# Attention scores from one product of 308 columns and two of 154, and a re-ordered slot, fill and end

## The chip, the cores and the metric

The kernel runs on one core of a Trainium2 chip. The metric is the device time of one launch in microseconds (us), lower is better; several executions of each kernel are timed and their median is compared. Besides, one execution was taken with the hardware profiler; the profile's numbers are of that execution.

## The reference, cut to what matters

Cross attention of `x` (32 batches, 512 queries, 640 channels) with a context of 77 rows of 1024 channels per batch, in 20 heads of 32 channels, float32 throughout. The text has 77 rows, so the object, other and image slices of the context are empty and only the text attention counts.

```python
q = heads(x @ to_q_w)                       # 32 x 20 x 512 x 32
k, v = heads(ctx @ to_k_w), heads(ctx @ to_v_w)   # 32 x 20 x 77 x 32
p = softmax(einsum('bhqd,bhkd->bhqk', q, k) / sqrt(32))
out = merge(einsum('bhqk,bhkd->bhqd', p, v)) @ to_out_w + to_out_b + x
```

## The kernel before

**Number format.** Every matrix product is done in the type fp32r. A float32 operand is first split into a high part (a cast to fp32r, ScalarE, `nc.scalar.copy`) and a low part (the rest, a subtraction, VectorE or GpSimd), and a product of two operands is the sum of three products, `PAIRS` (L127): high by high, high by low, low by high. A low by low product is left out. A product on TensorE (PE) is a weight load of a 128x128 tile (PEld) and a matmul that streams up to 512 columns through it into a PSUM bank.

**First stage** (to about 270 us): the keys and values of all batches are made from the context in column groups of 512, split, and written to DRAM: `k_dram` [128 channels, 5 chunks, 2 parts, 2464 keys] by `split_keys` (L207) and `v_dram`. The high part stands first. Two tiles `ks` take turns, and one DMA writes both parts of one chunk and group; it is issued by GpSimd, for the last group by SyncE (SP).

**Main stage**: 160 slots, `slot(n)` (L661). Slot n works for batch b = n // 5 and chunk j = n % 5; a chunk is 128 channels, that is 4 heads. A batch is thus 5 slots, j = 0 to 4. The order of all instructions on each engine is the order in which the program writes them (`manual_schedule`, L267); no scheduler moves them, and each engine takes its instructions in that order. In one slot there are, with the lines of the profile:

- scores for four blocks t of 128 queries, `scores(n, t)` (L448): three products of 308 columns (4 heads x 77 keys). The stationary operand is a block of the queries `qt` (parts high and low), the moving one is `kb`, which has the keys of head i in rows 32i to 32i+31 and columns 77i to 77i+76 and zeros elsewhere, in a high and a low copy. VectorE (DVE) takes the maximum of each head (L462).
- `exps(n, t)` (L467): four exponentials with their sums on ScalarE (ACT, L472).
- `queries(n + 1)` (L429): 15 products of 512 columns into the one bank `pq`; `split_q(n + 1)` (L443) casts it to `qt` on ACT (L103) and subtracts on DVE (L104). Two tiles `qt` take turns.
- `normalize(n - 1)` on GpSimd (POOL, L487), `transpose_p(n - 1)` on DVE (L494) and four DMAs from its output `z` to a scratch `pd` in DRAM; `load_p(n - 2)` loads it back in another layout as `raw` (L510, L511).
- for the slot that lies `LAG` = 3 back: `cast_p` (ACT, L518), `rest_p` (ACT L524 and DVE L525), `last_p` (POOL, L532), then `values` (six products of 512 columns into `pa`, L546), `sum_a` (ACT L557, DVE L559), and in the next slot `high_a` (ACT L566) and `low_a` (DVE L571).
- 24 products of 320 columns of the output projection of an earlier batch in two pieces, `piece` (L604, L589), into two banks `po` that take turns; `finish` (L612) adds each closed bank to the residual `xr` on DVE (L618), which frees the bank, and issues the DMA of a complete row block.
- `add_bias` (POOL, L582) on a loaded residual, at the places that `BIAS` (L635) names: j = 2, 3, 4 and 0.
- `refill` (L648): the keys or values of the next part, from SP's queue. `load_keys` (L411) issues one DMA for each head.
- the next batch's `x`: loads from SP, transposes on DVE (L256), and in j = 2 and 3 five splits (`split_x`, L258: ACT cast L263, POOL subtraction L264).

On ACT, DVE and POOL the order of a slot is, cut to what the prediction follows:

```
ACT : cast_p, high_a, rest_p, exps 0, exps 1, cast of qt, exps 2, [x casts], sum_a, [x casts], exps 3
POOL: last_p (waits for rest_p's cast), normalize(n - 1), [add_bias], [x subtractions]
DVE : rest_p, low_a, maxima 1 and 2, transpose_p(n - 1), low part of qt, maximum 3, finish, sum_a
PE  : scores 0, queries, scores 1, queries, scores 2, piece, values, scores 3, piece
```

In j = 3 the first piece and its `finish` stand ahead of `transpose_p`. Slots 3 to 6 are "filling": there is an older slot to take, but no projection yet; in these `cast_p`, `rest_p` and `last_p` follow `exps(n, 1)` and the first half of `refill` follows `load_p`.

**End**: `end()` (L771) takes the last three slots' values and projects what is left.

## Time and profile before

| | |
|---|---|
| median of 3 runs | 1954.53 us (1954.48 to 1955.75) |
| the profiled execution | 1951.98 us, span 1949.9 us, granted TensorE clock 0.994 |
| PE busy | 1905.3 us (98%), 10332 products |
| ACT, DVE, POOL busy | 1533.9, 1437.6, 1015.2 us (79, 74, 52%) |
| score products (L454) | 1920 of 128x308, mean 305 ns from start to modelled end |
| low part of `qt` (L104) | 160 of 128x512, mean 654 ns |
| cast of `qt` (L103) | 160 of 128x512, mean 598 ns |
| DMA | 431.28 MB, 560919 packets, 187024 of them under 512 B |

The profile has 40 slices of the span, groups of instructions by line, the waits of each engine with what ended them, and the instructions in order of time. A product's duration overlaps those of its neighbours, so the price of a product is read from one start to the next. SPq is SyncE's queue, which issues the DMAs; an issue there also takes time.

### The profile page before, as it was taken

What the parts mean: (1) busy time and instruction counts of PE and PEld (TensorE: products, weight loads), DVE (VectorE), ACT (ScalarE), POOL (GpSimd) and SP (SyncE); (2) the same over time, 40 slices, a digit from 0 to 9 for tenths busy, and PEclk for the clock granted to TensorE, in tenths of its full rate; (3) what the DMA queues carried; (4) which work ended last, traced back from release to release, by engine and by line L of the source; (5) the groups of instructions that cost most, each with busy time, mean ns of one, the idle gap of its engine ahead of it and who ended that gap; (6) DMA issues with size and microseconds to landing.
All of it is one profiled execution on the core that took longest, in us unless ns stands there. A gap on an engine that the chain in (4) does not pass through costs nothing.

```text
span 1949.9 us, 36251 instructions
## 1 busy us (share of the span) xinstructions
PE 1905.3 (98%) x10332; PEld 1701.3 (87%) x10332; DVE 1437.6 (74%) x2334; ACT 1533.9 (79%) x6210; POOL 1015.2 (52%) x668
## 2 busy tenths in 40 slices
PE   9999998999999999999999999999999999999997
PEld 7787896889889989988889989988989999888896
DVE  4444345887888788787888878788888888877874
ACT  3232237898988898888888888898989989888982
POOL 1100055566556655555556555566655665556543
PEclk9999999999999999999999999999999999999999
DMA  9878878888888888988888888888889888888874
GB/s 185 190 188 232 201 198 215 222 226 230 228 225 230 227 229 228 239 232 218 227 238 233 229 225 228 236 232 224 228 232 237 227 229 225 225 224 232 230 201 144
DMA packets 560919, 431.28 MB, mean 221 GB/s; under 512 B 187024, under 2 KB 469072, under 8 KB 560720
## 3 DMA queue, kind: packets, MB, share of 16 engines
q1 hardware_dynamic: 556208, 414.46, 82.3%
q0 software_dynamic: 4416, 14.34, 2.2%
q8 instruction: 84, 1.38, 0.3%
q14 instruction: 115, 0.94, 0.2%
q10 hardware_dynamic: 96, 0.16, 0.0%
HBM read 247.17 MB, written 181.64 MB: 220 GB/s over the span
## 4 chain that ended last, share of the span: by engine, by line
PE 20%; ACT 19%; issue 17%; DMA 15%; DVE 13%; POOL 12%; SPq 2%; DVEq 0%; POOLq 0%; ACTq 0%
ACT pn L472 10%; POOL pn L487 8%; DMA raw<-pd 7%; DMA pd<-z 6%; PE pq L435 5%; PE po L589 5%; POOL pp L532 4%; DVE pp L525 3%; ACT xt L263 3%; ACT aw L557 3%; PE pk L191 2%; PE pv L191 2%; PE sc L454 2%; DVE nm L462 2%; DVE z L494 2%
## 5 line engine op out<-in xcount | busy, mean ns | idle before, releaser
L472 ACT ACTIVATE pn<-sc,nm 128x77 f32<-128x77 f32 x2560 | 802.5, 335 | 70.9 <-DVE nm L462 68.0
L589 PE MATMUL po<-wo_s,at 128*128 128x320 f32 x3840 | 624.3, 310 | 17.7 <-DVE xr L618 14.4
L435 PE MATMUL pq<-xt,wq_s 128*128 128x512 f32 x2400 | 605.4, 393 | 0.0
L589 PEld LDWEIGHTS po<-wo_s,at 128*128 128x128 f32 x3840 | 575.4, 188 | 27.8 <-DVE xr L618 24.6
L532 POOL TENSOR_TENSOR pp<-raw,pp 64x512 fp32r<-64x512 f32 x160 | 211.8, 1324 | 643.6 <-ACT pp L524 413.4
L472 ACT ACTIVATION_READ_ACCUMULATOR pn<-sc,nm 128x1 f32 x2560 | 545.1, 213 | 0.0
L435 PEld LDWEIGHTS pq<-xt,wq_s 128*128 128x128 f32 x2400 | 436.8, 188 | 75.1
L454 PE MATMUL sc<-kb,qt 128*128 128x308 f32 x1920 | 377.5, 305 | 1.3 <-ACT pn L472 0.5
L487 POOL TENSOR_TENSOR pn<-pn,rs 128x1232 f32<-128x1232 f32 x160 | 364.4, 2277 | 24.7 <-DVE rs L482 12.6
L494 DVE STREAM_TRANSPOSE z<-pn 128x1280 f32<-128x1280 f32 x160 | 241.8, 1511 | 168.8 <-POOL pn L487 158.4
L454 PEld LDWEIGHTS sc<-kb,qt 128*128 128x128 f32 x1920 | 325.7, 189 | 45.0 <-ACT pn L472 1.6
L462 DVE TENSOR_REDUCE nm<-sc 128x4 f32<-128x308 f32 x640 | 295.1, 462 | 46.4 <-PE sc L454 44.1
L546 PE MATMUL pa<-pp,vb 128*128 128x512 f32 x960 | 256.0, 401 | 10.5 <-ACT pp L518 4.8
L525 DVE TENSOR_TENSOR pp<-raw,pp 128x1024 fp32r<-128x1024 f32 x160 | 195.6, 1222 | 88.2 <-ACT pp L518 78.9
L559 DVE TENSOR_TENSOR pa<-pa,aw 64x512 f32<-64x512 f32 x320 | 222.6, 696 | 34.7 <-ACT aw L557 25.2
L557 ACT COPY aw<-pa 64x1024 f32<-64x1024 f32 x160 | 162.0, 1012 | 79.6 <-PE pa L546 77.4
L264 POOL TENSOR_TENSOR xt<-xs,xt 128x512 fp32r<-128x512 f32 x160 | 204.3, 1296 | 37.1 <-ACT xt L263 35.3
L546 PEld LDWEIGHTS pa<-pp,vb 128*128 128x128 f32 x960 | 175.3, 190 | 43.8 <-ACT pp L518 5.8
L582 POOL TENSOR_TENSOR xr<-xr,bias 128x640 f32<-128x640 f32 x128 | 201.5, 1575 | 0.2
L518 ACT CAST pp<-raw 128x1024 fp32r<-128x1024 f32 x160 | 168.9, 1055 | 33.0 <-DMA raw<-pd 33.0
L191 PE MATMUL pk<-ct,wk_s 128*128 128x512 f32 (+1 forms) x600 | 137.9, 388 | 9.1 <-ACT ct L103 6.4
L191 PEld LDWEIGHTS pk<-ct,wk_s 128*128 128x128 f32 x600 | 114.2, 191 | 31.1 <-ACT ct L103 7.3
(43 smaller groups left out, 1358.0 us busy)
## 6 DMA issues: line engine op xcount, KB each, us to landing
pd<-z SPq DMA_DIRECT2D x640, 160.0 KB, 3.8
raw<-pd SPq DMA_DIRECT2D x160, 512.0 KB, 4.0
xs<-in_x_dram SPq DMA_DIRECT2D x128, 320.0 KB, 6.2
xr<-in_x_dram SPq DMA_DIRECT2D x128, 320.0 KB, 4.1
out_dram<-xr SPq DMA_DIRECT2D x127, 320.0 KB, 4.1
raw<-pd SPq DMA_DIRECT2D x160, 128.0 KB, 4.2
v_dram<-vs SPq DMA_DIRECT2D x80, 192.0 KB, 3.9
k_dram<-ks POOLq DMA_DIRECT2D x20, 512.0 KB, 3.7
```

The source lines that it names most:

```text
L191: nc.tensor.matmul(held[j][:, :gn], w[:, k, a, :], cts[g, k][:, c, :gn], start=(k == 0 and n == 0), stop=(k == NK - 1 and n == 2),)
L435: nc.tensor.matmul(pqs[n], wq_s[:, k, a, j * P : (j + 1) * P], xts[b, k][:, c, :], start=(k == 0 and m == 0), stop=(k == NC_ - 1 and m == 2),)
L454: nc.tensor.matmul(sc[:, :KCOLS], qt[:, a, t * P : (t + 1) * P], kb[:, j - GROUPS[g][0], c], start=(m == 0), stop=(m == 2),)
L462: nc.vector.tensor_reduce(nm, sc[:, :KCOLS].rearrange("p (h k) -> p h k", k=NKEY), AX.X, ALU.max, negate=True)
L472: nc.scalar.activation(pnb[n % 2][:, at, :NKEY], sc[:, i * NKEY : (i + 1) * NKEY], AF.Exp, bias=nm[:, i : i + 1], accum_out=sms[n][:, at : ...
L487: nc.gpsimd.tensor_tensor(pf, pf, rs.unsqueeze(2).to_broadcast([P, NQ * HPC, NKEY]), ALU.mult)
L494: nc.vector.transpose(z.rearrange("p b t j -> p t b j"), pn.rearrange("p (t h) k -> p t (h k)", t=NQ).rearrange("p t (b i) -> p t b i", i=Q),)
L525: nc.vector.tensor_tensor(pp[:, 2:4, :], raw[:, 0:2, :], pp[:, 0:2, :].bitcast(F32), ALU.subtract)
L532: nc.gpsimd.tensor_tensor(pp[64:, 4, :], raw[:64, 2, :], pp[:64, 4, :].bitcast(F32), ALU.subtract)
L546: nc.tensor.matmul(pas[n][:, p, :], vb[:, p, t, :], pp[:, c, :], start=(c == p), stop=(t == 1),)
L559: nc.vector.tensor_tensor(pa[64 * p : 64 * p + 64, 0], pa[:64, p], aw[:, p], ALU.add)
L589: nc.tensor.matmul(pos[b, t, h][:, :HALF], ats[b * NC_ + j][:, a, t * P : (t + 1) * P], wos[0][:, j, c, h * HALF : (h + 1) * HALF], start= ...
```

## The change

The high by low and the low by high product have the same rows half empty: rows of heads 0 and 1 meet only columns 0 to 153, rows of heads 2 and 3 only columns 154 to 307. The new score tile is one product of 308 columns (high by high, as before) and two of 154 columns: the first holds, for heads 0 and 1, the low queries in rows 0 to 63 and the high queries, copied, in rows 64 to 127, against a key tile `kc` with their high keys in rows 0 to 63 and their low keys in rows 64 to 127; the second does the same for heads 2 and 3 with the two halves of the rows exchanged. `qt` has three parts instead of two: the high queries and two mixed ones. GpSimd makes the two copies (64 rows by 512 columns each, to the other half of the partitions), and the subtraction on DVE becomes two of 64 rows.

`kb` keeps the high keys alone, `kc` holds both parts at half width: the bytes in SBUF are the same. `load_keys` issues two DMAs for each head. The two parts of `k_dram` now are the two pairs of heads, each with its high keys in one half of the rows and its low keys in the other, so `split_keys` issues three DMAs instead of one.

In a slot, `add_bias` is moved: for j = 2 and 3 (and in the last slot) ahead of `scores(n, 0)`, for j = 4 and 0 behind `split_q`. In j = 0, too, the first piece and its `finish` now come ahead of `transpose_p`. In the filling slots `cast_p`, `rest_p` and `last_p` stand where the other slots have them. In `end()`, `piece(last - 1, 6)` with its `finish` is moved to the start and `transpose_p(N - 1)` behind the second `finish`.

```diff
@@ -209,9 +209,10 @@
         ks = kvt.tile([P, 2, G], FPR, tag="ks", name="ks")
         split(ks[:, 0, :gn], ks[:, 1, :gn], pks.pop(j)[:, :gn])
         engine = nc.gpsimd if g + 1 < len(GROUPS_KV) else nc.sync
-        engine.dma_start(
-            k_dram[:, j, :, g0 : g0 + gn].bitcast(F32), ks[:, :, :gn].bitcast(F32)
-        )
+        dst = k_dram.rearrange("(h r) c w n -> r c w h n", h=2)[:, j, :, :, g0 : g0 + gn]
+        engine.dma_start(dst[:, 0].bitcast(F32), ks[:64, :, :gn].bitcast(F32))
+        for half in range(2):
+            engine.dma_start(dst[:, 1, half].bitcast(F32), ks[64:, 1 - half, :gn].bitcast(F32))
 
     def values_of(g, j, pool):
 
@@ -394,14 +395,16 @@
     nc.sync.dma_start(bias, bo.unsqueeze(0).to_broadcast([P, C]))
     kbs, vbs, pnb = [], [], []
     for g, (j0, nj) in enumerate(GROUPS):
-        kb = main.tile([P, nj, 2, KCOLS], FPR, name=f"kb{g}")
-        nc.gpsimd.memset(kb.bitcast(F32), 0.0)
-        kbs.append(kb)
+        kb = main.tile([P, nj, KCOLS], FPR, name=f"kb{g}")
+        kc = main.tile([P, nj, 2, KCOLS // 2], FPR, name=f"kc{g}")
+        for tile_ in (kb, kc):
+            nc.gpsimd.memset(tile_.bitcast(F32), 0.0)
+        kbs.append((kb, kc))
     for n in range(2):
         pn = main.tile([P, NQ * HPC, KPAD], F32, name=f"pn{n}")
         nc.gpsimd.memset(pn, 0.0)
         pnb.append(pn)
-    qts = [main.tile([P, 2, S], FPR, name=f"qt{n}") for n in range(2)]
+    qts = [main.tile([P, 3, S], FPR, name=f"qt{n}") for n in range(2)]
     z = main.tile([P, NBLK, NQ, Q], F32, name="z")
     for g, (j0, nj) in enumerate(GROUPS):
         vb = main.tile([P, nj, 2, 2, P], FPR, name=f"vb{g}")
@@ -410,10 +413,14 @@
 
     def load_keys(b, g, heads=range(HPC)):
         j0, nj = GROUPS[g]
+        kb, kc = kbs[g]
         src = k_dram[:, j0 : j0 + nj, :, b * NKEY : (b + 1) * NKEY].bitcast(F32)
         for i in heads:
-            r = slice(i * HD, (i + 1) * HD)
-            nc.sync.dma_start(kbs[g][r, :, :, i * NKEY : (i + 1) * NKEY].bitcast(F32), src[r])
+            r, half = slice(i * HD, (i + 1) * HD), i % 2 * NKEY
+            nc.sync.dma_start(
+                kb[r, :, i * NKEY : (i + 1) * NKEY].bitcast(F32), src[r, :, i // 2, :]
+            )
+            nc.sync.dma_start(kc[r, :, :, half : half + NKEY].bitcast(F32), src[r])
 
     def load_values(b, g, segments=SEGMENTS):
         j0, nj = GROUPS[g]
@@ -443,18 +450,34 @@
     def split_q(n):
 
         qt, pq = qts[n % 2], pqs.pop(n)
-        split(qt[:, 0, :], qt[:, 1, :], pq)
+        nc.scalar.copy(qt[:, 0, :], pq)
+        lower, upper = slice(0, 64), slice(64, P)
+        halves = ((lower, upper), (upper, lower))
+        for w, (r, other) in enumerate(halves):
+            nc.gpsimd.tensor_copy(qt[other, 1 + w, :], qt[r, 0, :].bitcast(F32))
+        for w, (r, other) in enumerate(halves):
+            nc.vector.tensor_tensor(
+                qt[r, 1 + w, :], pq[r], qt[r, 0, :].bitcast(F32), ALU.subtract
+            )
 
     def scores(n, t):
         b, j = divmod(n, NC_)
         g = GROUP_OF[j]
-        qt, kb = qts[n % 2], kbs[g]
+        qt, (kb, kc) = qts[n % 2], kbs[g]
+        jg = j - GROUPS[g][0]
         sc = ps.tile([P, S], F32, tag="sc", name="sc", bufs=3)
-        for m, (a, c) in enumerate(PAIRS):
+        half = KCOLS // 2
+        for m, (cols, keys_) in enumerate(
+            (
+                (slice(0, KCOLS), kb[:, jg]),
+                (slice(0, half), kc[:, jg, 0]),
+                (slice(half, KCOLS), kc[:, jg, 1]),
+            )
+        ):
             nc.tensor.matmul(
-                sc[:, :KCOLS],
-                qt[:, a, t * P : (t + 1) * P],
-                kb[:, j - GROUPS[g][0], c],
+                sc[:, cols],
+                qt[:, m, t * P : (t + 1) * P],
+                keys_,
                 start=(m == 0),
                 stop=(m == 2),
             )
@@ -672,15 +695,18 @@
         filling = taken is not None and not has_out
         if not filling:
             refill(b, j, 0)
-        if taken is not None and not filling:
+        if taken is not None:
             cast_p(taken)
         if n - 1 in takes:
             high_a(takes[n - 1])
+        bias_now = j in BIAS and b >= BIAS[j][0]
+        if bias_now and (j in (2, 3) or not ahead):
+            add_bias(b - BIAS[j][0], BIAS[j][1])
         s = scores(n, 0)
-        if taken is not None and not filling:
+        if taken is not None:
             rest_p(taken)
         rs = sums(n - 1) if n else None
-        if taken is not None and not filling:
+        if taken is not None:
             last_p(taken)
         if n:
             normalize(n - 1, rs)
@@ -704,13 +730,7 @@
             load_x(b + 2, (0, 1))
         if j in RESIDUAL and b >= RESIDUAL[j][0]:
             load_residual(b - RESIDUAL[j][0], RESIDUAL[j][1])
-        if j in BIAS and b >= BIAS[j][0]:
-            add_bias(b - BIAS[j][0], BIAS[j][1])
         exps(n, 1, *s)
-        if filling:
-            cast_p(taken)
-            rest_p(taken)
-            last_p(taken)
         for i in turns[0]:
             transpose_x(b + 1, i)
         if ahead:
@@ -720,13 +740,16 @@
             exps(n, 2, *s)
             piece(bo_, first)
             s = scores(n, 3)
-        if j == 3 and has_out:
+        early = ahead and has_out and j in (0, 3)
+        if early:
             piece(bo_, first)
             finish()
         if n and has_out:
             transpose_p(n - 1)
         if ahead:
             split_q(n + 1)
+            if bias_now and j not in (2, 3):
+                add_bias(b - BIAS[j][0], BIAS[j][1])
             exps(n, 2, *s)
         if n and not has_out:
             transpose_p(n - 1)
@@ -743,7 +766,7 @@
             sum_a(taken)
             return
         if has_out:
-            if j != 3:
+            if not early:
                 piece(bo_, first)
         else:
             s = scores(n, 3)
@@ -773,17 +796,17 @@
 
         last = B - 1
         load_p(N - 2)
-        transpose_p(N - 1)
+        piece(last - 1, 6)
+        finish()
         high_a(N - 4)
+        cast_p(N - 3)
         low_a(N - 4)
-        cast_p(N - 3)
         rest_p(N - 3)
         last_p(N - 3)
         add_bias(last - 1, 3)
-        piece(last - 1, 6)
-        finish()
         piece(last - 1, 7)
         finish()
+        transpose_p(N - 1)
         load_p(N - 1)
         load_residual(last, 0)
         load_residual(last, 1)
```

## The prediction

> **What bounds the kernel now.** I read the page first, then the stretches of the span, the waits in the steady part (420 to 1850 us), and the instructions of single slots in order of time.
>
> ```profile
> PE 1905.3 (98%) x10332; PEld 1701.3 (87%) x10332; DVE 1437.6 (74%) x2334; ACT 1533.9 (79%) x6210; POOL 1015.2 (52%) x668
> ```
>
> ```profile
> 420.00:1850.00 1430.00, 1421.48 (x7993) 1285.25 (x7993) 1153.84 (x1881) 1279.23 (x5332) 851.07 (x535) 1.00 0.87 229
> ```
>
> ```profile
> DVE z L494 <- POOL pn L487: 142.3, 129, 2.0
> ...
> ACT pp L518 <- DMA raw<-pd: 31.1, 28, 2.3
> PEld po L589 <- DVE xr L618: 16.1, 29, 1.2
> ```
>
> The second line has the busy us of PE, PEld, DVE, ACT and POOL in the steady part: PE 1421 of 1430. A batch has 285 products (75 + 60 + 120 + 30), so 7993 of them are 28.05 batches of 50.98 us. The last three lines (waits: us, times, longest) say that PE is not alone: once a batch it waits for a bank (0.57 us; without it PE would need 50.4), and once a batch the first cast of a slot waits 1.1 us for `raw`. So a second thing runs at nearly PE's pace. It is seen in one slot with j = 1: ACT and POOL, then DVE, then PE.
>
> ```profile
> 899.28 1.05 ACT L518 CAST pp<-raw 128x1024 fp32r<-128x1024 f32 x1 [1.81 <-DMA raw<-pd]
> ...
> 901.46 1.29 POOL L532 TENSOR_TENSOR pp<-raw,pp 64x512 fp32r<-64x512 f32 x1 [6.60 <-ACT pp L524]
> ...
> 902.83 2.27 POOL L487 TENSOR_TENSOR pn<-pn,rs 128x1232 f32<-128x1232 f32 x1
> ...
> 907.64 0.33 ACT L472 ACTIVATE pn<-sc,nm 128x77 f32<-128x77 f32 x1 [0.84 <-DVE nm L462]
> ...
> 908.86 1.06 ACT L518 CAST pp<-raw 128x1024 fp32r<-128x1024 f32 x1
> ```
>
> ```profile
> 905.14 1.51 DVE L494 STREAM_TRANSPOSE z<-pn 128x1280 f32<-128x1280 f32 x1 [0.95 <-POOL pn L487]
> 906.57 0.65 DVE L104 TENSOR_TENSOR qt<-pq,qt 128x512 fp32r<-128x512 f32 x1
> 907.15 0.46 DVE L462 TENSOR_REDUCE nm<-sc 128x4 f32<-128x308 f32 x1
> ```
>
> ```profile
> 905.27 0.59 PE L454 MATMUL sc<-kb,qt 128*128 128x308 f32 x3
> 905.71 1.93 PE L589 MATMUL po<-wo_s,at 128*128 128x320 f32 x12
> 907.47 0.59 PE L454 MATMUL sc<-kb,qt 128*128 128x308 f32 x3
> 907.90 1.55 PE L435 MATMUL pq<-xt,wq_s 128*128 128x512 f32 x6
> ```
>
> This is a ring: casts of `raw` on ACT (899.28 to 901.46: 2.18), `last_p` (1.37), normalise (2.31), transpose (1.43), low part of `qt` (0.58), maximum 3 (0.49), exponentials 3 (1.22), and the next slot's cast at 908.86. Each step starts as the one before ends; the sum is 9.58. The maximum had its scores at about 905.9 and still waited for the subtraction ahead of it on DVE. The next casts start at 919.20, 929.52, 939.11 and 950.42 (the last after 1.62 of waiting for `raw`): steps of 10.34, 10.32, 9.59 and 9.69. In j = 3 ACT's casts of x come last, with 0.8 to spare for the maximum; in j = 2 up to 0.3. The ring without its `raw` wait is 49.5 us a batch against PE's 50.4, and with it 51.1.
>
> **Part by part.**
>
> *Score products.* From start to start in the rows above: 308 columns (907.90 - 907.47)/3 = 0.143, 320 columns 1.76/12 = 0.147. With 0.231 for 512 columns (15 in a slot), a column costs 0.44 ns, and 154 columns would cost 75 ns. But each has its own weight load, and where PE restarts after a wait, loads follow one another faster than products:
>
> ```profile
> 307.99 0.19 PEld L454 LDWEIGHTS sc<-kb,qt 128*128 128x128 f32 x1 [0.79 <-ACT pn L472]
> 308.10 0.19 PEld L454 LDWEIGHTS sc<-kb,qt 128*128 128x128 f32 x1
> 308.24 0.19 PEld L454 LDWEIGHTS sc<-kb,qt 128*128 128x128 f32 x1
> ```
>
> The second load starts 0.11 after the first though PE was idle: no row shows loads closer than this. I take 0.115 for a product of 154 columns, with ends 0.075 and 0.231 (the widest row; nothing under 308 columns is in the trace, so dearer than 308 is not excluded). A score tile goes from 0.429 to 0.143 + 2 x 0.115 = 0.373, and 640 tiles take 36 us off PE (87 at 0.075, 45 at 0.108; 111 us more at 0.231); PE would need 50.4 - 20 x 0.056 = 49.3 a batch. The Trainium skill, "TensorE: Matmul & The Clock Gate", section "Back-to-back issue gap", gives columns/2.4 + 2.5 ns for the isolated gap, 67 ns for 154 columns, which would make it 82 us; the row for 308 columns (143 where the rule has 131) and the 0.11 between loads speak against it.
>
> *Two subtractions for one.* A half-height instruction isn't cheaper: 64x512 on DVE has a mean of 696 ns (L559), 128x512 of 654 (L104). So 160 more, at 0.58 from start to start (906.57 to 907.15), all on the ring ahead of maximum 3. The ring becomes 9.58 + 0.58 in j = 1, the same more in j = 4 and 0, 0.33 to 0.58 in j = 2, nothing in j = 3: 49.5 + 2.1 to 2.3 = 51.6 to 51.8 a batch. Nothing hides it: queued behind are maximum 3, `finish` and `sum_a`; ACT's exponentials and the next cast wait for the maximum. ACT's own work is unchanged.
>
> *Copies on GpSimd.* Two of 64x512, one input. From below, a memset (128x1280 in 1167 ns) gives 0.47; from above, L532 (two inputs, 64x512, also from one half of the partitions to the other) 1.32. I take 0.9 each. They stand behind normalise, ready at 905.14 above, and end at 906.9 (907.8 at the upper end); the second subtraction ends at about 907.8. So they end no later than DVE. In j = 3 POOL then has 1.6 (bias) + 1.3 + 2.3 + 1.8 + 3 x 1.3 = 10.9, 11.7 at most, in a slot of 10.3; its excess is covered by the wait ahead of the next `last_p` (6.60 above). Cost zero. The Trainium skill, "GPSIMD Engine Reference", section "Elementwise — side-by-side cycle accounting", has 1.8 cycles an element as the best case, an estimate of 0.77 for a copy, inside the two rows; no row here shows a copy.
>
> *Bias.* Ahead of `scores(n, 0)` it falls into POOL's same wait before `last_p`; behind `split_q` POOL is free until then. Zero; without that cover, 1.6 a slot on the ring.
>
> *Key loads.* 256 more issues on SP, eight a batch in j = 0 and 2, and half as much again of key packets: 20480, which at the page's mean (82.3% of 16 engines' 1950 us over 556208 packets, 46 ns) is 3% of DMA time at most. In j = 2 SP waits for `pd` behind the first key issues, so two more are covered. In j = 0 they are not: SP is in one run from the `pd` issues (936.92) over x, output and two key DMAs (941.83, 1.88) to the load of `raw` (943.88), the one that the cast at 950.42 waited for. Two more cost 0 to 1.2 there (1.22 for two in a calmer batch). The longer ring gives the load 1.16 in j = 4 and 0, the size of its present wait, so the excess shows: I take 0.5.
>
> *Banks.* The early `finish` in j = 0 uses DVE's idle 0.95 ahead of the transpose and takes the 0.57 off PE. With the ring as the bound this only adds to PE's room.
>
> *Steady sum.* Ring 51.7 + 0.5 = 52.2 against 50.98: +1.2 a batch, 30 batches: +36 us. Ends: 51.6, nothing from SP, +0.6, +18; 51.7 + 1.2 = 52.9, +1.9, +58.
>
> *First stage and fill.* Three issues for one, 0.73 each on POOL (L212), while that engine waits 198 us for `ks`; covered. For the last group they are on SP, ahead of eight key issues that become sixteen (7.88 us for eight): up to 5 late. The four filling slots leave PE idle for some 13 us at L546, because `cast_p` is late; the earlier cast may give back 0 to 13, I take 8. Net -5 (+5 to -13).
>
> *End.* PE stands for 6.1 us at 1906 to 1912 because `finish` on DVE is queued behind the transpose, which waits for `z` until 1908.6. Moved ahead, it goes at once, and the transpose still starts at 1908.6. -5 (0 to -8), since the last slots' casts then set the end.
>
> Sum: +36 - 5 - 5 = +26; from -3 to +63. The profiled execution of 1951.98 would become 1978; the median is 2.5 above it, so 1980.
>
> **The rivals.**
>
> *PE stays the bound (faster).* If the ring has room that the one batch hides, the steady part falls to PE's 49.3: -36 from the scores, -17 from the bank wait (0.57 x 30), -10 from fill and end: 1892 (1883 at 0.108). For it: the x casts give slack in two of five slots, and PE is busy 99%. Against: three steps without any slack, and 2 us added to a ring that was 0.9 short of PE. It decides only if the added DVE work is under some 0.25 a slot.
>
> *Narrow products are dear (slower still).* At 0.231 each, PE needs 50.4 + 20 x 0.176 = 53.9 a batch and leads again: +2.9 x 32 - 10 = +83, 2038. It decides from 0.19 on, where PE needs 52.2. For it, only that no row is under 308 columns; against it, the load's 0.11.
>
> *Nothing moves.* A ring of 51.6 with all of the gain in fill and end: 1954 + 18 - 21 = 1951.
>
> **How the numbers follow.** Less than 0.2% (4 us) can hardly be told from no change. Forecast 0.57 (1950 to 2015 by its ends; 0.02 of it faster by over 0.2%), PE as the bound 0.22, dear narrow products 0.14, nothing moves 0.07. Faster 0.24, same 0.07, slower 0.69. The range takes in the forecast's ends and the first rival down to 1884; the dear products and the rival's tail stay out.
>
> **What would show it.** Right: PE's busy share falls in the steady part; maximum 3 starts about 0.58 later after the transpose; casts lie 10.15 apart in j = 1, 4 and 0; a batch takes 52 us; the wait of L518 for `raw` stays near 1 us a batch; the bank wait is gone; weight loads of the 154-column products start 0.11 to 0.12 apart. Wrong: a batch under 50.9 with DVE idle between transpose and maximum 3, or loads 0.19 or more apart and PE still at 99%.

## The result: slower by 4%, and the profile after

The changed kernel takes 2032.7 us (median), the kernel before 1954.5 us beside it: a ratio of 1.040 (95% interval 1.038 to 1.042). The profiled execution took 2031.54 us (span 2029.8), 79.6 more than the 1951.98 of before. The forecast was 1980 and its upper end 2015: the right sign, a third of the size.

First the line of busy times on the page, and the stretch from 420 to 1900 us (busy us of PE, PEld, DVE, ACT, POOL):

```profile
PE 1913.5 (94%) x10332; PEld 1677.6 (83%) x10332; DVE 1559.7 (77%) x2494; ACT 1533.9 (76%) x6210; POOL 1237.7 (61%) x1030
```

```profile
420.00:1900.00 1480.00, 1409.89 (x7915) 1247.40 (x7914) 1246.15 (x1999) 1266.44 (x5279) 1022.19 (x807) 1.00 0.88 223
```

PE was busy 99% of the steady part and is now at 95% at a full granted clock; it no longer sets the pace. The waits of the same stretch (us, times, longest) say who does:

```profile
ACT pn L495 <- DVE nm L485: 188.9, 250, 1.9
DVE z L517 <- POOL pn L510: 182.0, 139, 1.7
...
PE sc L477 <- DVE qt L459: 46.5, 115, 0.9
...
PEld po L612 <- DVE xr L641: 5.4, 15, 1.2
ACT pp L541 <- DMA raw<-pd: 4.0, 6, 1.2
```

The exponentials wait 189 us for DVE's maxima (54 before, the longest 0.9), and PE now waits for the subtractions L459. The bank wait fell from 16.1 us, and the wait of the first cast for `raw` from 31.1 us to 4.0: the loop of casts, normalise and DVE has grown so long that both are early. One slot with j = 1, in order of time (start, duration, idle before):

```profile
989.75 1.06 ACT L541 CAST pp<-raw 128x1024 fp32r<-128x1024 f32 x1
...
999.23 0.33 ACT L495 ACTIVATE pn<-sc,nm 128x77 f32<-128x77 f32 x1 [1.68 <-DVE nm L485]
...
1000.44 1.06 ACT L541 CAST pp<-raw 128x1024 fp32r<-128x1024 f32 x1
```

```profile
995.87 1.51 DVE L517 STREAM_TRANSPOSE z<-pn 128x1280 f32<-128x1280 f32 x1 [0.94 <-POOL pn L510]
997.31 1.37 DVE L459 TENSOR_TENSOR qt<-pq,qt 64x512 fp32r<-64x512 f32 x2
998.71 0.48 DVE L485 TENSOR_REDUCE nm<-sc 128x4 f32<-128x308 f32 x1
```

The casts lie 10.69 apart, not 9.58. Between transpose and maximum 3, from the first subtraction on, it is 1.40 us (997.31 to 998.71) where it was 0.58 (906.57 to 907.15). That is the ring of the forecast, lengthened on the forecast's own spot by 0.82 instead of 0.58. Means over 22 batches, in us from the first cast of a slot to that of the next:

| slot j | before | after | longer by (raw wait of before taken off) | forecast |
|---|---|---|---|---|
| 0 | 10.92, of it 1.07 raw wait | 10.65 | 0.80 | 0.58 |
| 1 | 9.68 | 10.62 | 0.94 | 0.58 |
| 2 | 10.47 | 11.16 | 0.69 | 0.33 to 0.58 |
| 3 | 10.32 | 10.47 | 0.15 | 0 |
| 4 | 9.58 | 10.42 | 0.84 | 0.58 |
| batch | 50.97 | 53.32 | 3.42 - 1.07 = 2.35 | |

Where the 80 us of span are, by the starts of the slots: slot 0 starts 9.9 later (282.1 against 272.2), slots 0 to 9 take 5.6 more, the 28 batches behind them 64.1 (53.296 - 51.007 each), the last ten slots to the start of slot 159 3.6, and from there the end takes 3.3 less.

### The profile page after: what moved, and what is told of

Its sections match the earlier page's. It is cut to its first block, busy times and chain, and to the rows that moved or that the text cites. A ratio compares the mean times of both kernels' runs of the same rounds, so it can differ in the third digit from the quotient of the medians.

```text
span 2029.8 us, 37658 instructions
## 1 busy us (share of the span) xinstructions
PE 1913.5 (94%) x10332; PEld 1677.6 (83%) x10332; DVE 1559.7 (77%) x2494; ACT 1533.9 (76%) x6210; POOL 1237.7 (61%) x1030
## 4 chain that ended last, share of the span: by engine, by line
POOL 24%; DVE 19%; DMA 18%; issue 13%; ACT 12%; PE 11%; SPq 3%; DVEq 0%; POOLq 0%; ACTq 0%
POOL pn L510 14%; POOL pp L555 9%; PE pk L191 6%; DVE qt L459 6%; DMA raw<-pd 5%; DMA pd<-z 5%; ACT pn L495 4%; DVE z L517 4%; DMA xs<-in_x_dram 3%; DVE pa L582 3%; ACT pp L541 3%; PE pv L191 3%; DVE nm L485 2%; ACT at L589 2%; DMA out_dram<-xr 2%
## 5 line engine op out<-in xcount | busy, mean ns | idle before, releaser
L612 PE MATMUL po<-wo_s,at 128*128 128x320 f32 x3840 | 641.6, 315 | 5.9 <-DVE xr L641 3.1
L442 PE MATMUL pq<-xt,wq_s 128*128 128x512 f32 x2400 | 620.3, 399 | 0.0
L442 PEld LDWEIGHTS pq<-xt,wq_s 128*128 128x128 f32 x2400 | 429.7, 190 | 76.1
L555 POOL TENSOR_TENSOR pp<-raw,pp 64x512 fp32r<-64x512 f32 x160 | 216.2, 1352 | 387.6 <-ACT pp L547 279.3
L477 PE MATMUL sc<-kc,qt 128*128 128x154 f32 x1280 | 257.8, 263 | 79.8 <-DVE qt L459 50.4
L477 PEld LDWEIGHTS sc<-kc,qt 128*128 128x128 f32 x1280 | 218.4, 188 | 131.6 <-issue 69.3
L459 DVE TENSOR_TENSOR qt<-pq,qt 64x512 fp32r<-64x512 f32 x320 | 214.5, 670 | 9.5 <-ACT qt L453 4.6
L457 POOL CAST qt<-qt 64x512 fp32r<-64x512 f32 x320 | 195.4, 611 | 19.7
L477 PE MATMUL sc<-kb,qt 128*128 128x308 f32 x640 | 195.9, 306 | 9.0 <-ACT pn L495 4.3
```

Source lines behind the costliest of these rows:

```text
L442: nc.tensor.matmul(pqs[n], wq_s[:, k, a, j * P : (j + 1) * P], xts[b, k][:, c, :], start=(k == 0 and m == 0), stop=(k == NC_ - 1 and m == 2),)
L459: nc.vector.tensor_tensor(qt[r, 1 + w, :], pq[r], qt[r, 0, :].bitcast(F32), ALU.subtract)
L477: nc.tensor.matmul(sc[:, cols], qt[:, m, t * P : (t + 1) * P], keys_, start=(m == 0), stop=(m == 2),)
L555: nc.gpsimd.tensor_tensor(pp[64:, 4, :], raw[:64, 2, :], pp[:64, 4, :].bitcast(F32), ALU.subtract)
L612: nc.tensor.matmul(pos[b, t, h][:, :HALF], ats[b * NC_ + j][:, a, t * P : (t + 1) * P], wos[0][:, j, c, h * HALF : (h + 1) * HALF], start= ...
```

## The experiments

The theory on trial, the ring: the chain from the cast through normalise, transpose, subtraction and maximum 3 to the next cast sets the time, and the second subtraction is the term that lengthens it. Rivals: the copies on GpSimd hold PE; the earlier bias or the longer key queue does; narrow products are dear. Ratios are to the kernel before on the same chip, with 95% intervals.

**The second subtraction alone.** To the kernel before:

```diff
-        split(qt[:, 0, :], qt[:, 1, :], pq)
+        nc.scalar.copy(qt[:, 0, :], pq)
+        for r in (slice(0, 64), slice(64, P)):
+            nc.vector.tensor_tensor(qt[r, 1, :], pq[r], qt[r, 0, :].bitcast(F32), ALU.subtract)
```

> The kernel before, with its one low-part subtraction of 128 rows made as two of 64 rows, nothing else. Ring theory (the ring cast, last_p, normalise, transpose, subtraction, maximum 3, exponentials 3 sets the pace, and the second subtraction lengthens it): a batch goes from 50.99 to 52.7 - 53.3 us, the time to 2008 - 2026. Rival A (GpSimd's copies) and rival B (the doubled key issues on SP): neither is in this kernel, so a batch stays within 0.3 of 50.99 and the time within 10 us of before.

2051.4 us, 1.049 (1.047 to 1.050), 54.1 us a batch: slower even than the whole change. The waits from 420 to 1800 us show that the longer ring meets the bank:

```profile
PEld po L593 <- DVE xr L622: 63.3, 26, 2.5
PE po L593 <- DVE xr L622: 56.5, 26, 2.3
```

Once a batch, 2.2 to 2.4 us, PE stands until `finish` behind DVE's longer chain frees it. The wait costs more than its length. In the trace the granted TensorE clock is 0.5 for 3.4 us behind 20 of these 26 waits (0.975 over the run); six products of the projection there take 1.66 us instead of 1.04, three of the scores 0.97 instead of 0.59:

```profile
553.20 1.66 PE L593 MATMUL po<-wo_s,at 128*128 128x320 f32 x6 [2.16 <-DVE xr L622]
554.65 0.97 PE L458 MATMUL sc<-kb,qt 128*128 128x308 f32 x3
```

With the change's early `finish` besides:

```diff
-        if j == 3 and has_out:
+        early = ahead and has_out and j in (0, 3)
+        if early:
             piece(bo_, first)
             finish()
```

> The kernel before with two subtractions (54.1 a batch) and with the first piece and its finish ahead of the transpose in j = 0. Theory (with the late finish PE stands 2.2 us a batch for a bank and the casts of j = 1 come late with it; the subtractions alone make 52.8 - 53.2): a batch 52.8 - 53.3, the time 2008 - 2028, the bank wait under 0.3. Rival (the excess over the kernel after is the dearer score products): a batch stays over 53.8.

2018.5 us, 1.032 (1.030 to 1.033), 53.06 us a batch: **the key run**. The bank wait is 1.7 us in all, and the casts by slot lie 10.49, 10.64, 11.10, 10.41 and 10.41 apart against the changed kernel's 10.65, 10.62, 11.16, 10.47 and 10.42. Wide products, no copies, the old key loads and the old bias, and yet 2.06 of the 2.29 us a batch are there; of the span's 80 us this run shows 67. It also sizes the early banks, 1.08 us a batch once DVE's chain is long; as the granted clock is 1.00 in the steady part of this run, the 1.08 are the wait and the lowered clock together.

**What of it is dear: half height, two of them, or the partitions?** To the kernel above, the two halves replaced by the 128-row subtraction written twice:

```diff
+        for _ in range(2):
+            nc.vector.tensor_tensor(qt[:, 1, :], pq, qt[:, 0, :].bitcast(F32), ALU.subtract)
```

> The kernel before with its 128-row subtraction written twice (the second repeats the first and computes nothing new), and the first slot finishing its banks early. Tells whether the price of the second subtraction comes from the half height or from there being two: if two neighbours of 64 rows cost 1.41 us because half-height operations do not overlap as a 128-row one does, two of 128 rows take about 1.2 us from the first start to maximum 3, the batch 52.3-52.6 and the run 1990-2005 us. If any second subtraction costs its whole 0.67-0.70 us, the start of maximum 3 is 1.35-1.45 us behind the first subtraction, the batch 53.0-53.1 and the run 2015-2022 us, as with two halves.

1996.2 us, 1.022 (1.021 to 1.024), 52.36 us a batch. DVE in a slot of this kernel, then in one with two halves:

```profile
964.48 1.38 DVE L448 TENSOR_TENSOR qt<-pq,qt 128x512 fp32r<-128x512 f32 x2
965.77 0.47 DVE L464 TENSOR_REDUCE nm<-sc 128x4 f32<-128x308 f32 x1
```

```profile
961.88 1.35 DVE L448 TENSOR_TENSOR qt<-pq,qt 64x512 fp32r<-64x512 f32 x2
963.26 0.48 DVE L466 TENSOR_REDUCE nm<-sc 128x4 f32<-128x308 f32 x1
```

From first subtraction to maximum: 1.29 and 1.38, against 0.58 with one. The batch falls where half height by itself would put it, but 1.29 is neither the 1.2 of that case nor the 1.35 of the other, so height is not shown to be the answer. In the kernel with two of 128 rows both write the same tile, and in its trace the second carries a wait for the first; in the one with halves each starts on other partitions than the operation before it, and the second carries no wait. Two more runs take these apart, each with a second subtraction into a tile of its own that nothing reads. Two of 128 rows:

```diff
+        for low in (qt[:, 1, :], spare_q[:, :]):
+            nc.vector.tensor_tensor(low, pq, qt[:, 0, :].bitcast(F32), ALU.subtract)
```

> The kernel with the 128-row subtraction twice and the early banks, its second one now writing a tile of its own that nothing reads. If the second waited for the first only because both wrote the same tile, it now starts 0.56-0.60 us behind the first, the maximum 1.14-1.20 behind the first (1.29 with one tile), and the batch is 51.8-52.2 us, the run 1975-1990. If a subtraction behind a subtraction always starts 0.68 behind, nothing changes: 1.29, 52.3-52.4 us a batch, 1992-2000 us. The Trainium skill, VectorE: DVE Perf Modes, section Two Vector instructions with no wait between them, has an instruction start early unless its inputs or output start in another quarter of the partitions than those before; by it alone the first case holds.

Two of 64 rows, both on the lower rows:

```diff
+        r = slice(0, 64)
+        for low in (qt[r, 1, :], spare_q[r, :]):
+            nc.vector.tensor_tensor(low, pq[r], qt[r, 0, :].bitcast(F32), ALU.subtract)
```

> The kernel with two subtractions of 64 rows and the early banks, both now on the lower 64 rows, the second into a tile of its own that nothing reads (the low part of the upper rows is left out and stays zero). If it is the change of partitions that holds an operation until the one before has ended, the second starts 0.56-0.60 us behind the first and the maximum 1.14-1.20 behind the first, the batch takes 51.8-52.2 us and the run 1975-1990. If half height as such is dear, the pair stays at 1.36-1.42 us, the batch at 53.0-53.1 and the run at 2014-2022 us.

1984.8 us, 1.015 (1.012 to 1.017), and 1983.8 us, 1.014 (1.012 to 1.016); both 51.85 us a batch. DVE in a slot of the second:

```profile
959.54 0.65 DVE L452 TENSOR_TENSOR qt<-pq,qt 64x512 fp32r<-64x512 f32 x1
960.11 0.67 DVE L452 TENSOR_TENSOR spare_q<-pq,qt 64x512 fp32r<-64x512 f32 x1
960.71 0.45 DVE L468 TENSOR_REDUCE nm<-sc 128x4 f32<-128x308 f32 x1
```

0.57 and 0.60 apart, 1.17 to the maximum, in both kernels. That settles the price. Half height costs nothing by itself and a subtraction overlaps a subtraction as a maximum does; what costs is the step from the lower rows to the upper ones and back: the second half waits for the first to end, and the maximum for the second. Of the 2.06 us a batch 0.84 come from there being a second subtraction (51.85 - 51.01; the ring grows by more, as the wait for `raw` ahead of j = 1 falls from 1.07 to 0.19) and 1.21 from its starting on other partitions (53.06 - 51.85). Into the same tile the second of two 128-row subtractions is held as well, by its wait for the first: 0.5 a batch (52.36).

**The change without its second subtraction** (one of 64 rows; the low part of the upper heads is left out):

```diff
-        for w, (r, other) in enumerate(halves):
-            nc.vector.tensor_tensor(
-                qt[r, 1 + w, :], pq[r], qt[r, 0, :].bitcast(F32), ALU.subtract
-            )
+        nc.vector.tensor_tensor(
+            qt[lower, 1, :], pq[lower], qt[lower, 0, :].bitcast(F32), ALU.subtract
+        )
```

> The kernel after without its second subtraction: the low queries of heads 2 and 3 are left out (zeros stand there). Copies, narrow products and key loads stay. Ring theory: the ring loses 0.7 a slot, PE needs about 48.3, and what is left is the load of raw in j = 0: a batch 49.8 - 51, the time 1940 - 1975. Rivals A and B: a batch stays at 52.5 or more, the time over 2005.

A miss: 2015.5 us, 1.031 (1.029 to 1.032), 52.8 us a batch. The ring did go back in j = 1 and 4 (9.57 and 9.58, as before), but j = 0, 2 and 3 took 11.32, 11.37 and 10.94. The waits from 420 to 1800 us show what came in its place:

```profile
POOL xr L606 <- DMA xr<-in_x_dram: 58.0, 19, 4.7
ACT pp L542 <- DMA raw<-pd: 42.9, 26, 3.1
```

The wait for `raw` is back with 1.65 us a batch (1.1 before). The early bias waits for its residual about as long as in the changed kernel (63.9 us of the same stretch), but now `last_p`, queued behind it on GpSimd, is late: in j = 2 it starts 3.50 us behind the first cast, where it is 2.76 in the changed kernel and 2.60 before, and in j = 3 it lasts 1.81 us instead of 1.29.

**The copies.** The two GpSimd copies taken out (the high queries of the correction are then zero):

```diff
-        for w, (r, other) in enumerate(halves):
-            nc.gpsimd.tensor_copy(qt[other, 1 + w, :], qt[r, 0, :].bitcast(F32))
```

> The kernel after without GpSimd's two copies a slot (the high queries beside the low ones are left out, zeros stand there). Ring theory: the copies end before the second subtraction, so a batch stays at 53.1 - 53.4 and only the fill gives back 1 to 4 us: 2024 - 2032. Rival A: a batch falls under 52, the time under 1995.

2032.3 us, 1.040 (1.038 to 1.041), 53.4 us a batch: the copies cost nothing in this kernel. That rival is out.

**The subtractions apart**: the first ahead of the transpose, in DVE's idle time, the second behind maximum 3:

```diff
+        if ahead:
+            split_q(n + 1, (0,))
         if n and has_out:
             transpose_p(n - 1)
         if ahead:
-            split_q(n + 1)
...
             s = scores(n, 3)
+            split_q_low(n + 1, 1)
```

> The kernel after, complete, with another order on VectorE: the first subtraction ahead of the transpose (where VectorE waits for GpSimd), the second behind maximum 3. No work is taken out. Ring theory: no subtraction is left in the ring, 9.1 - 9.2 in j = 1, 4, 0; then ScalarE in j = 2 and 3, the load of raw or PE (48.3) lead: a batch 48.5 - 50.8, the time 1890 - 1960. Rivals A and B: a batch stays at 52.5 or more.

A miss as well: 2022.7 us, 1.034 (1.033 to 1.036). Again the ring does what it should (9.0 and 9.19 in j = 1 and 4), and again j = 0, 2 and 3 lose it (11.74, 11.92, 11.19), on the same two waits: `raw` 51.0 us, bias for `xr` 73.6 us. So the bias was put behind the copies in every slot:

```diff
-        if bias_now and (j in (2, 3) or not ahead):
+        if bias_now and not ahead:
             add_bias(b - BIAS[j][0], BIAS[j][1])
...
-            if bias_now and j not in (2, 3):
+            if bias_now:
                 add_bias(b - BIAS[j][0], BIAS[j][1])
```

> The kernel with the two subtractions set apart (53.05 a batch), and every bias addition behind GpSimd's copies. Theory 2 for this order (once the subtractions are out of the ring, the early bias waits for its residual's load and holds last_p by 1 to 1.9 us in j = 2 or 3): a batch 51.0 - 51.8, the time 1955 - 1985. Theory 3 (DMA in general or ScalarE sets the pace there): a batch stays over 52.6.

2003.3 us, 1.025 (1.022 to 1.027), 52.4 us a batch, between the two expectations: the bias wait is gone and 19 us with it, but j = 0 still takes 11.5, of it 1.8 for `raw`. Issuing j = 0's first key loads behind the load of `raw`:

```diff
-        if not filling:
+        if not filling and j:
             refill(b, j, 0)
...
-        if filling:
+        if filling or not j:
             refill(b, j, 0)
```

> As apart_bias_late, and in j = 0 the first key issues stand behind the load of raw in SP's queue. Theory (the eight key issues of j = 0 delay raw, for which the first cast of j = 1 waits about 2 us): the wait falls to 1 or less, a batch 50.0 - 51.0, the time 1925 - 1960, faster than apart_bias_late by 20 to 40. Rival (the wait is the transfer of x beside it, not the queue): no change over 8 us.

2027.6 us, 1.037 (1.034 to 1.041): the wrong way. The waits for `raw` nearly doubled (87.8 us, 65 times, against 47.4 us, 26 times) and now come in j = 1 too (10.44 instead of 9.0); the queue only moved its lateness.

**The early bias by itself**: the changed kernel with the bias of j = 2 and 3 back behind normalise:

```diff
-        if bias_now and (j in (2, 3) or not ahead):
-            add_bias(b - BIAS[j][0], BIAS[j][1])
         s = scores(n, 0)
...
             load_residual(b - RESIDUAL[j][0], RESIDUAL[j][1])
+        if bias_now and (j in (2, 3) or not ahead):
+            add_bias(b - BIAS[j][0], BIAS[j][1])
         exps(n, 1, *s)
```

> The kernel after with the additions of the bias of j = 2 and 3 back behind normalise. Theory 1 (the two subtractions make the ring of after long enough that the early bias is done before last_p is due): a batch stays at 53.0 - 53.4, the time 2024 - 2034. Theory 2 (the early bias waits for its residual and holds last_p in after as well): a batch falls to 52.5 or less, the time under 2010.

2051.5 us, 1.049 (1.047 to 1.050), which neither theory expected: 0.7 us a batch worse. In j = 4 the ring takes 11.34, with 2.22 between the starts of `last_p` and normalise instead of 1.37, and PE waits for the copies:

```profile
PEld sc L477 <- POOL qt L457: 42.1, 78, 0.7
PE sc L477 <- POOL qt L457: 28.2, 78, 0.5
```

With copies, bias and x's low parts in one slot, GpSimd is busy until `last_p` of j = 4 is due. That `last_p` starts only 0.06 us later, but it lasts 2.14 us instead of 1.29, which is the 0.85; why it lasts longer right behind the low parts of x is not shown. So the early bias is not a cost as long as the ring is long: without it the changed kernel is slower.

**All three limits away**: one subtraction, the bias late, and the wide key tile loaded for batch 0 only (later batches keep its keys).

```diff
+            if b == 0:
                 nc.sync.dma_start(
                     kb[r, :, i * NKEY : (i + 1) * NKEY].bitcast(F32), src[r, :, i // 2, :]
                 )
             nc.sync.dma_start(kc[r, :, :, half : half + NKEY].bitcast(F32), src[r])
```

> The changed kernel with one subtraction of 64 rows (the low part of the upper heads left out), the bias behind the copies in every slot, and the wide key tile loaded in batch 0 alone (later batches keep its keys), so that j=0 and j=2 issue four key transfers, not eight. If the second subtraction, the longer key queue and the early bias are together what holds the changed kernel back, each covering for the others, the batch falls to 50-51 us, the raw wait in j=0 to under 1 us, and the run to 1935-1970 us. If something else of the change holds it (the product tiles, the copies, the banks), the batch stays at 52 or more: 2000-2015 us.

1972.2 us, 1.010 (1.008 to 1.012), 51.5 us a batch: between the two expectations. The wait for `raw` is 20.8 us, 0.8 a batch, and j = 1 is at 9.57. What is left sits in j = 4 (10.57 instead of 9.58), on GpSimd:

```profile
1045.33 1.56 POOL L607 TENSOR_TENSOR xr<-xr,bias 128x640 f32<-128x640 f32 x1
1046.85 3.79 POOL L265 TENSOR_TENSOR xt<-xs,xt 128x512 fp32r<-128x512 f32 x3
1050.72 2.16 POOL L557 TENSOR_TENSOR pp<-raw,pp 64x512 fp32r<-64x512 f32 x1
```

The low parts of x end at 1050.64, and `last_p` runs back to back behind them. In j = 4 it starts 0.13 us later behind the first cast than before, and again lasts 2.16 us instead of 1.29: together the 1.0. It may be that the copies' 1.3 us a slot, free in the changed kernel, have a price once the ring is short; no run tests that.

**The narrow products alone**, on the kernel before (each correction reaches half of the heads only):

```diff
+            cols = (slice(0, KCOLS), slice(0, h), slice(h, KCOLS))[m]
             nc.tensor.matmul(
-                sc[:, :KCOLS],
+                sc[:, cols],
                 qt[:, a, t * P : (t + 1) * P],
-                kb[:, j - GROUPS[g][0], c],
+                kb[:, j - GROUPS[g][0], c, cols],
```

> The kernel before with its score products of 308, 154 and 154 columns and nothing else of the change (each correction is added to half the heads only). If TensorE gains the 2 us a batch that the starts show, its own time falls from 50.4 to 48.4, the ring with the raw wait (49.5 and some 0.5 to 1.1) sets the batch at 50.0-50.6 instead of 51.0, and the run takes 1926-1944 us. If the ring was already all of the 51.0, the run is the same within 4 us, 1950-1958. If narrow products free nothing on TensorE, also the same, but then the idle time in front of PE's products does not grow by 2 us a batch.

1949.9 us, 0.998 (0.997 to 0.999), 50.8 us a batch, between the expectations and nearest to the second. PE's busy time from 420 to 1800 us falls from 1371.8 to 1348.6 us, and the waits of the same stretch show where the gain went (15.5 and 6.7 us before):

```profile
PEld po L591 <- DVE xr L620: 39.3, 31, 1.9
...
PE po L591 <- DVE xr L620: 31.1, 28, 1.6
```

PE reaches the bank earlier and waits there: 0.9 us a batch more (both lines tell of the same waits). Alone, the tiles shorten a batch by 0.2 us.

**A shorter ring from the kernel before**: its one 128-row subtraction behind maximum 3, the early banks and the new end; then the same with narrow products.

```diff
         else:
             s = scores(n, 3)
+            split_q_low(n + 1)
...
         if has_out:
             s = scores(n, 3)
+            split_q_low(n + 1)
         finish()
```

> The kernel before with its one 128-row subtraction moved behind maximum 3, the batch's first slot finishing its banks early, and the new end. Ring theory (the chain from pp's cast through normalise, transpose, subtraction and maximum 3 to the next cast sets the time): the ring falls to about 9.1 us in j=1 and j=4 and the batch from 51.0 to 50.0-50.6, where TensorE's own 50.4 us takes over; with 3 to 7 us off the end 1930-1948 us in all. Rival (other limits lie so close that a shorter ring only meets the raw wait and the residual's transfer, as in the kernel with the subtractions apart): batch 51 or more, raw wait in j=0 over 1.5 us, 1950-1975 us.

> The kernel with the subtraction behind maximum 3, the early banks and the new end, with score products of 308, 154 and 154 columns besides (each correction added to half the heads only). If TensorE's own time sets the 50.8 us of that kernel without narrow products, the batch falls to 48.8-49.8 and the run to 1890-1915 us. If the transfers and the order of ScalarE set it (raw wait in j=0, exponentials 3 behind the casts of the value sums in j=2 and j=3), the batch stays at 50.4-50.8 and the run at 1930-1942 us, with the gain turned into PE's waits.

1941.8 us, 0.994 (0.992 to 0.996), and 1939.9 us, 0.992 (0.991 to 0.994). Both beat both kernels, and they do not differ: 50.79 and 50.80 us a batch, the first between its two expectations, the second as its own second one has it. By slot the casts lie 11.55, 8.99, 10.92, 10.31 and 8.99 apart in the first, and within 0.11 of that in the second. PE's narrower tiles buy nothing there. What the short slots 1 and 4 gave is taken in j = 0, where the wait for `raw` (44.9 and 53.7 us from 420 to 1800 us) is 1.7 and 2.0 us a batch, and in j = 2 and 3, where exponentials 3 start 0.8 and 1.4 us behind the end of their maximum because ScalarE is still at the work queued ahead of them.

**The fill.** Each key tile of the first stage written with one transfer instead of three (the upper heads' high and low keys are then not exchanged), and the clearing of the value tiles moved:

```diff
-        dst = k_dram.rearrange("(h r) c w n -> r c w h n", h=2)[:, j, :, :, g0 : g0 + gn]
-        engine.dma_start(dst[:, 0].bitcast(F32), ks[:64, :, :gn].bitcast(F32))
-        for half in range(2):
-            engine.dma_start(dst[:, 1, half].bitcast(F32), ks[64:, 1 - half, :gn].bitcast(F32))
+        engine.dma_start(
+            k_dram[:, j, :, g0 : g0 + gn].bitcast(F32), ks[:, :, :gn].bitcast(F32)
+        )
...
-        nc.gpsimd.memset(vb.bitcast(F32), 0.0)
...
     split_q(0)
+    for vb in vbs:
+        nc.gpsimd.memset(vb.bitcast(F32), 0.0)
```

> The changed kernel with the fill's two suspects taken away: each key tile of the first stage written to DRAM with one transfer instead of three (the upper heads' high and low keys are then not exchanged), and the clearing of the value tiles issued behind slot 0's copies. If these are the +9.9 us that slot 0 starts later than before, it starts at 272-274 us instead of 282.1, and the run is 2021-2025 us with the batch at 53.3 as before. If only the queue of GpSimd before slot 0 matters, slot 0 starts at 277-278 us, the run 2027-2029; if neither, 282 us and no change.

2021.7 us, 1.035 (1.033 to 1.038); slot 0 starts at 273.4, the batch stays at 53.3. 8.7 of the 9.9 us are these two, which the run does not separate. In the changed kernel GpSimd and PE around slot 0 stood like this:

```profile
278.45 2.27 POOL L411 MEMSET vb<- 128x1024 f32 x2 [7.88 <-DMA k_dram<-ks]
280.79 1.28 POOL L457 CAST qt<-qt 64x512 fp32r<-64x512 f32 x2
```

```profile
282.08 0.50 PE L477 MATMUL sc<-kb,qt 128*128 128x308 f32 x1 [4.11 <-POOL qt L457]
```

The clearing waits for the key tiles, whose memory it takes over, and the first copies are queued behind it. The rest is in the first stage: before, one write per key tile; after, three, and ScalarE's casts of the next tiles wait for their landing (8.7 us from 255 to 300 us against 3.9 without).

## Why the prediction was wrong

*The bound and its mechanism held.* The ring sets the pace, PE's share fell, the bank wait went, the copies (0.611 us each, forecast 0.9) cost nothing, and the time rose. PE was hardly what held the kernel before, either: with narrow products alone it has less to do and a batch falls by 0.2 us only.

*The failed step is the price of the second subtraction*: 0.58 "from start to start (906.57 to 907.15)", where the runs show 0.82. The 0.58 is right for an operation on the same partitions (0.57 and 0.60 in the runs), and with it the batch takes 51.85, just above the forecast's 51.6 to 51.8 for the ring and below its 52.2 with SP's share. But the two halves start on different partitions, which holds the second and the maximum behind it: 1.40 instead of 1.17. A row that points to it was in the trace before, two 64x512 operations in a row that write lower and then upper rows:

```profile
959.92 1.43 DVE L559 TENSOR_TENSOR pa<-pa,aw 64x512 f32<-64x512 f32 x2
961.26 0.46 DVE L462 TENSOR_REDUCE nm<-sc 128x4 f32<-128x308 f32 x1
```

From their first start to the operation behind them it is 1.34, and 1.34 - 0.58 = 0.76 a slot, near what the ring gained (0.84 in j = 4, 0.80 in j = 0). The likeness is not complete: the second one there carries a wait for the first, and the maximum behind it is not held (0.61 from start to start). The prediction used the mean of L559 only to say that half height is not cheaper. The Trainium skill, "VectorE: DVE Perf Modes", section "Two Vector instructions with no wait between them", states it as a rule, which it calls a model: an instruction whose inputs or output start in another quarter of the partitions than those of the instructions before is held until these have finished. The runs agree: 0.68 and 0.72 apart across the halves, each start 0.03 behind the end of the one before; 0.57 and 0.60 without a change, where the next starts before that end.

*Slots 1, 2 and 3.* Forecast 0.58, 0.33 to 0.58 and 0, measured 0.94, 0.69 and 0.15. ScalarE's casts of x covered what the picture had shown: in the means of before, exponentials 3 start 0.41 (j = 2) and 0.77 us (j = 3) behind the end of maximum 3, after 0.04 in both. But they cover that much of 0.83, not of 0.58, which leaves 0.46 and 0.10. The rest, 0.23 in j = 2 and 0.20 in j = 1, lies between the first cast and normalise: ScalarE's cast of `at`, queued ahead of the one that `last_p` needs, starts 0.17 and 0.11 later behind it. In j = 2 it waits for the value sums, which stand behind maximum 3 on DVE (0.45 us, 0.29 before). In all 3.42 us a batch instead of the 2.2 (2.1 to 2.3).

*The ring's start.* 49.5 was read off one batch; the mean without the wait for `raw` is 50.97 - 1.07 = 49.90. Another 0.4 a batch.

*The wait for `raw`.* Forecast +0.5 from SP's longer run, measured nearly none left (0.2 a batch): a ring that is longer in every slot gives the load more time than two more key issues cost. The longer slots (3.42 - 2.2), the ring's start and this wait together are 1.2 + 0.4 - 0.5 = 1.1 us a batch, the difference between 53.3 and the forecast 52.2. Where the ring was shortened the wait came back (1.65 to 2.0 us a batch), so the step's mechanism is real and its sign here was wrong.

*Narrow products.* By the starts of single products in the steady part: 0.142 us behind 308 columns, 0.072 between the two of 154, 0.112 before the next product's start (medians), 0.33 a tile, where the forecast had 0.143 + 2 x 0.115 = 0.373. So they are cheaper than priced, and the rival "narrow products are dear" is out. The loads in a tile start 0.141 and then 0.108 apart and none nearer, close to the 0.11 of the row at 308 us, but the products do not keep that distance one by one. The section "Back-to-back issue gap" of the Trainium skill's "TensorE: Matmul & The Clock Gate", which the prediction set aside, gives by its formula for the isolated gap an estimate of 67 ns for 154 columns: near the 72 between the two, too low for the 112 behind the second. (The prediction's 111 us for products at 0.231 is 113 by its own figures, 640 x 0.176; nothing rests on it.) The tile's price decided nothing: PE was not the bound.

*The fill.* Forecast -5, measured +9.9 up to slot 0 and +5.6 in slots 0 to 9. "That engine waits 198 us for `ks`; covered" was the error for the first stage: the three writes delay not GpSimd but the buffers that ScalarE's casts wait for. And the copies brought GpSimd, which was off the path there, in front of slot 0, behind a clearing that waits for a transfer. The gain expected from earlier casts in the filling slots appeared only as 0.8 us up to slot 7; then slot 7, where the first early bias waits 7.6 us for its residual with `last_p` behind it, takes 16.2 us instead of 10.5. Without that bias it takes 12.5, but slots 7 to 9 together 38.0 us where the changed kernel takes 37.8, so its wait is not shown to be the cause of the 5.6 us; with two subtractions alone slots 0 to 9 already take 2.9 more.

*The bias.* "Zero" as long as POOL waits anyway was right in the long ring, by luck of its length: the change without it is slower, and with a shorter ring it costs 19 us.

*The end.* Forecast -5, measured -3.3.

What stays open: the last 0.23 us a batch between two subtractions with early banks and the whole change, why `last_p` lasts up to 2.16 us when it follows other work on GpSimd closely, and which of the transfers holds 50.8 us a batch once the ring is shorter.

## What to carry to other kernels

Price an added operation by a row in which the same neighbours meet: what follows it decides how much of it is hidden. When two limits lie within 2% of each other, a gain on one (PE's 2 us a batch) turns into a wait on the next (bank, transfer, `raw`), and a change that pays for it on the other is a loss; count a whole loop's mean, not one batch's picture. Removing the term that made a kernel slower need not make it fast again: behind it stood two more waits that it had hidden. A half-height operation costs a full one, and lower and upper halves in turn cost more: splitting work over partition halves to feed a cheaper product is paid for twice on DVE.

## What the runs showed of the hardware

On DVE, 64x512 and 128x512 subtractions last 0.65 to 0.67 us alike. The next operation starts 0.57 to 0.61 after the start of one on the same partitions, 0.66 to 0.73 after one on other partitions, and 0.69 when it writes the same tile again and carries a wait for that. On TensorE, products of 154 columns follow each other 0.072 us apart, and the next product starts 0.112 after the last of them. In one run (two subtractions, late banks) TensorE's granted clock was 0.5 for 3.4 us behind 20 of 26 waits of 2.1 to 2.3 us in the steady part. On GpSimd the two-input operation `last_p` lasted 1.29 us (medians over all runs, 420 to 1800 us) when it began over 1 us behind the end of the operation before it, 1.76 at 0.3 to 0.6 us and 2.16 at under 0.1 us; the reason is open. A GpSimd copy of 64x512 from one half of the partitions to the other takes 0.611 us, less than half of the two-input operation of the same size (1.35).
